# Nine z buffers, three spreads of each kind, and new prices in the planner of a one-core scan, attention and expert kernel

## The chip, the cores and the metric

The kernel runs on one core of a Trainium2 chip. The metric is the device time of one execution in microseconds (us); for a kernel that was run several times it is the median of the runs. Beside the times there is one profiled execution, and everything that is said of single instructions comes from it.

## The reference, cut to what matters

The input x has 4 batches of 384 channels and 32 x 32 positions. Layer 0 is a selective scan in four directions over the 1024 positions; layer 1 is windowed attention followed by a mixture of four experts, of which two serve each token. All numbers are float32.

```
# layer 0, per batch, direction k, channel d, state n (16 states):
dt = softplus(dt_rank @ dt_w + bias)               # time steps
h[l] = h[l-1] * exp(dt[l] * A) + (dt[l] * u[l]) * B[l]
y[l] = sum over n of h[l] * C[l]                   # then four directions are merged,
x = x + gelu(layernorm(merged y + D * u))
# layer 1, per token:
t = t + attention(layernorm(t))                    # 6 heads, causal window of 64
t = t + sum over 2 of 4 experts: gate * (gelu(ln(t) @ w1 + b1) @ w2 + b2)
```

## The kernel before, in words

**The scan.** The 384 channels are cut into 3 tiles of 128 and each tile into 4 blocks of 32 channels. One scan instruction works on 128 partitions (32 channels times 4 states) by 1024 positions, so a block of 32 channels takes 4 *slots* (`NG`), one for each group of 4 states, and the whole kernel 768 slots: 4 batches, 4 directions, 12 blocks, 4 groups. The slots alternate between the two blocks of a pair: `place_of` puts slots 0, 2, 4, 6 of eight in one block and 1, 3, 5, 7 in the other. A slot goes through these steps, each a generator in the code:

- `spread` loads, for each block, two *spreads* from DRAM by a DMA of 512 KB on SyncE's queue: the time steps dt (buffers `dts`) and dt times u (buffers `dtu`, printed in the profile as `dts` too), each row repeated for the four states.
- `times_b` (GpSimd): z = dtu spread times B. It takes a z buffer from the stock `zs_` and may be at most `AHEAD` = 3 slots in front of the scans.
- `decay` (ScalarE): dA = exp(dts spread times A), into one of two PSUM buffers.
- `scan` (VectorE): the recurrence over z and dA.
- `times_c`: the product with C, either on GpSimd, in place in z (`z<-z,bc`), or on VectorE, from PSUM (`z<-dA,bc`). Which it is depends, at planning time, on whether GpSimd's clock in the plan is behind VectorE's by enough.
- `fold_y` (TensorE): sums the four states of a channel by a product with the matrix `fold`, for pairs of slots; then the z buffers are free again.

`time_steps` computes the dt (products `ps_dt`, then ScalarE and VectorE) some 40 slots before they are needed.

**The rest.** As soon as a batch's scans are folded, `tokens` runs its 8 token tiles (norms, attention), then `route` sorts tokens by expert, and `experts` runs 19 *expert blocks* of 128 rows for each batch: 36 products `ps_hid`, 12 gelu activations and 12 products `y_ff`, with the weights loaded from DRAM. `combine` gathers the two experts' rows. Batch b's layer 1 lies beside the scans of the batches after it. What is left of layer 1 after the last scan runs by itself.

**What sets the order.** A planner written in the kernel (`Machine`) runs all generators against a model of the engines before anything is built. Each instruction that a generator yields gets a price from `Engine.ask`; `Machine.choose` picks, on the engine that is free first, the instruction with the smallest ready time plus bias. Biases are `EARLY` (-6), none (the scan chain) or `LATER` (+6, the experts). For TensorE, `account` also keeps a book of work in windows of 3.413 us and stretches a price by `COLD` = 1.9 when the last window had little. The result is one fixed program for each engine. On the chip the engines and SyncE's DMA queue run their programs in order and wait for one another by semaphores; so the prices change nothing on the chip but the order, and who does the second product and the copies.

`settled` holds a generator back until the planned write of a tile lies at most `SOON` ahead.

The prices that the change touches stand in `Engine.ask`: products with 32 output rows are the folds, products with under 32 input rows are the time steps `ps_dt`, and `act` is ScalarE.

Buffers are handed out by `Stock.take` and `Stock.give`, first free first used. At the end of the scans the z, dtu and dts buffers, 15 in all before and after, are given to the stock of rows.

Of the kernel before, what the change touches and what calls it, by code (L numbers as in the profile page):

```python
# [17 lines left out]
P = 128  # L18
B, D, HH, WW = 4, 384, 32, 32
L = HH * WW  # L20
# [22 lines left out]
HID_RANK = 2  # L43
GELU_BIAS = EARLY
FAVOUR = 1.0
TILES, EPS, NZ = 3, 1e-5, 7
CORES = 1
NEG = -1.0e30

# [80 lines left out]
class Engine:  # L130
# [23 lines left out]
    def ask(self, op, a, k):  # L154
        aps = [v for v in list(a) + [v for n, v in k.items() if n not in ("out", "accum_out")] if hasattr(v, "tensor")]
        if "out" in k:
            outs, ins = [k["out"]], aps
        else:
            outs, ins = aps[:1], aps[1:]
        if op == "value_load":  # L160
            outs, ins = [], aps
        if op == "tensor_tensor_reduce":
            outs, ins = outs + ins[-1:], ins[:-1]
        if k.get("accum_out") is not None:
            outs = outs + [k["accum_out"]]
        for v in list(k.values()):
            if isinstance(v, bass.IndirectOffsetOnAxis):
                ins = ins + [v.ap]
        n = max(v.free_size() if callable(v.free_size) else v.free_size for v in (outs if op == "matmul" else outs + ins))
        size, table = 0, None  # L170
        if "dma" in op:
            size = max(_nbytes(v) for v in outs + ins[:1])
            if op == "indirect_dma_start":
                size = P * D * 4
            cost = dict(pool=1.0, act=0.38, sp=0.48)[self.name]
        elif self.name == "pe":
            cost = max(n, 122) * (0.00088 if op == "transpose" else 0.00176)
            if outs[0].shape[0] == 32:
                cost = 0.01 + 0.00022 * n
            if ins[0].shape[0] < 32:  # L180
                cost *= 0.6
        elif self.name == "act":
            cost = 0.08 + 0.00085 * n + 0.1 * sum(hasattr(k.get(v), "tensor") for v in ("bias", "scale"))
            cost += 0.19 if "accum_out" in k else 0.0
            table = TABLES.get(a[2]) if op == "activation" else None
        elif self.name == "pool":
            cost = 0.1 + 0.0022 * n
        elif self.name == "sp":
            cost = 1.5
        else:  # L190
            cost = 0.17 + 0.00198 * n if "scan" in op else 0.14 + 0.00105 * n
            if n < 256 and not any(v.space == PSUM for v in outs + ins):
                cost += 0.5
        asked = Op(self.name, outs, ins, cost, table, size)
        if self.name == "pe":
            asked.work = cost * min(ins[0].shape[0], P) / P if outs[0].shape[0] > 32 else 0.5 * cost
        return asked


def _nbytes(ap):  # L200
    n = 4
    for s in ap.shape:
        n *= s
    return n
# [6 lines left out]
class Machine:  # L211
# [42 lines left out]
            t = max(t, r + (HOP if e != eng else 0.0))  # L254
        return t

    def settled(self, *tiles):

        names = [ap.tensor.name for ap in tiles]
        return lambda: max(self.written.get(n, (0.0, None))[0] for n in names) <= self.t + SOON  # L260

    def account(self, op, start):
        e = op.eng
# [103 lines left out]


PATIENCE = 3.0
SOON = 0.5  # L370
WINDOW, COLD = 3.413, 1.9
MARGIN, QUEUES = 1.0, ("sp",)

# [3 lines left out]
def conv_attn_hybrid(  # L377
# [89 lines left out]
    m = Machine(nc)  # L467
# [41 lines left out]
    work = ctx.enter_context(tc.tile_pool(name="work", bufs=1))  # L509
    rp = ctx.enter_context(tc.tile_pool(name="rp", bufs=2))  # L510
    zs_ = Stock(m, work, "z", NZ, [P, L])
    dtus, dts = (Stock(m, work, n, 4, [P, L]) for n in ("dtu", "dts"))
    bs_, cs_ = (Stock(m, work, n, 4, [P, L]) for n in ("rb", "rc"))
    rows = Stock(m, work, "row", NROW, [P, D])
    xbs, xbts, hss, ybs = (
# [38 lines left out]
    def place_of(s):  # L554

        return s // SP * 2 + s % 2, s % SP // 2
# [280 lines left out]
    def times_c(s, h, on_pool):  # L837
        n, g = place_of(s)
        i = blocks[n][0]
        yield lambda: (i, g, 1) in bcs  # L840
        if on_pool:
            yield from pool.tensor_tensor(zs[s], zs[s], bcs[i, g, 1], ALU.mult)
        else:
            yield from dve.tensor_tensor(zs[s], h, bcs[i, g, 1], ALU.mult)
            das_.give(h)
        if n % NB == NB - 1:
            cs_.give(bcs.pop((i, g, 1)))
        ready.add(s)

    def scan():  # L850

        for s in range(NSLOT):
            n, g = place_of(s)
            i = blocks[n][0]
            yield lambda: s in zs and s in das
            z, da = zs[s], das.pop(s)
            on_pool = count_of["times"] >= min(s + AHEAD, NSLOT) and m.clock["pool"] < m.clock["dve"] + LEAD
            h = z if on_pool else da
            if turns[i][1] >= 2:
                yield from dve.tensor_tensor_scan(  # L860
                    h[:, ::-1], da[:, ::-1], z[:, ::-1], 0.0, ALU.mult, ALU.add
                )
            else:
                yield from dve.tensor_tensor_scan(h, da, z, 0.0, ALU.mult, ALU.add)
            count_of["scan"] = s + 1
            if s % SP == 0:
                m.spawn(fold_y(n), EARLY)
            if on_pool:
                das_.give(da)
                m.spawn(times_c(s, h, True))  # L870
            else:
                yield from times_c(s, h, False)
        ended.append(True)
        yield lambda: len(das_.free) == 2
        for stock in (banks, ybank):
            stock.free.append(das_.free.pop(0))
        for stock, n in ((zs_, NZ), (dts, 4), (dtus, 4)):
            yield lambda: len(stock.free) == n
            rows.free += stock.free
            stock.free = []  # L880
# [3 lines left out]
    def fold_y(n):  # L884


        i, t, j = blocks[n]
        b, k = turns[i]
        rows_y = ydr[b][t, j : j + 2].rearrange("j r l -> (j r) l")
        prev = yield from yps.take("yp")  # L890
        yield from sp.dma_start(prev, rows_y)
        ps = None
        for g in range(NG):
            s = n // 2 * SP + 2 * g
            yield lambda: s in ready and s + 1 in ready
            pair = zs[s], zs[s + 1]
            yield m.settled(*pair)
            mm = Calls()
            if ps is None:
                ps = yield from banks.take("ps_y", 0)  # L900
            for n_z, z in enumerate(pair):
                for h in range(2):
                    if k % 2:
                        rhs = z.rearrange("p (w h) -> p w h", h=HH)[:, :, ts(h, HH // 2)]
                    else:
                        rhs = z[:, ts(h, LH)]
                    q = 32 * (2 * n_z + h)
                    mm.matmul(ps[q : q + 32, :], fold, rhs, start=g == 0, stop=g == NG - 1)
            yield from pe.all(mm)
            zs_.give(zs.pop(s), zs.pop(s + 1))  # L910
        yield from dve.tensor_tensor(prev, ps, prev, ALU.add)
        if k == LAST_BY_COLUMNS:
            yield from act.copy(
                ps.rearrange("p (h w) -> p w h", w=WW), prev.rearrange("p (w h) -> p w h", w=WW)
            )
            yield from act.copy(prev, ps)
        banks.give(ps)
        yield from sp.dma_start(rows_y, prev)
        yps.give(prev)
        folded[b] = folded.get(b, 0) + 2  # L920
        if folded[b] == KG * NB:
            have.add(("scan", b))
# [553 lines left out]
    with tc.manual_schedule():  # L1476
        for b in range(B):
            m.spawn(group_norm(b), EARLY)
        for gen in (turn_loads(), time_steps(), state_rows(0), state_rows(1), spread(1), spread(0)):
            m.spawn(gen, EARLY)  # L1480
        for gen in (decay(), times_b(), scan()):
            m.spawn(gen)
        m.spawn(layer1(), EARLY)
        for gen in (prepare(), mixture()):
            m.spawn(gen, LATER)
        m.run()
# [54 lines left out]
```

## Time and profile before

| | us |
|---|---|
| three runs | 4078.01, 4080.3, 4070.57 |
| median | 4078.01 |
| the profiled execution | 4065.49 |
| its span, first to last instruction | 4063.8 |
| busy in the span: TensorE, VectorE, GpSimd, ScalarE | 3014.8, 2878.0, 2855.7, 2432.7 |

PE is TensorE's matmul, PEld its weight loads, DVE is VectorE, ACT ScalarE, POOL GpSimd, and SPq SyncE's DMA queue. Tiles are printed as output<-inputs. A group of instructions is shown with its count, its busy time and the mean duration of one in ns. Waits are named by the engine that waited and by what ended the wait. The busy shares are means over the whole span; the kernel has stretches with different limits, so they have to be read by stretches. The first scan starts at 104.1 us and the last ends at about 3140 us. The groups with the most time of the scan chain are:

| group | count | mean ns |
|---|---|---|
| POOL z<-dts,bc (first product) | 768 | 2358 |
| DVE scans, into dA and into z | 393 and 375 | 2288 and 2276 |
| POOL z<-z,bc (second product) | 375 | 2356 |
| DVE z<-dA,bc (second product) | 393 | 1221 |
| ACT dA<-dts,a (decay) | 768 | 1116 |
| ACT table loads | 388 | 1283 |

### The profile page before, as it was taken

To read this page: it belongs to the slowest core of one execution; us is meant where nothing else is said; L and a number is where in the kernel's file an instruction comes from. 1 tells how busy PE (TensorE), PEld (TensorE's weight loads), DVE (VectorE), ACT (ScalarE), POOL (GpSimd) and SP (SyncE) were. 2 spreads that over 40 slices of the span, in tenths; PEclk is the share of its full clock that TensorE was granted. 3 is DMA by queue.
4 is the path that set the end of the run, shared out by engine and by line. 5 is a ranking of instruction groups with operands and counts; after the bars stand their busy time and mean duration, and the time that the engine had idled before them with its cause. 6 is when DMAs were issued, how large, how long until landed. Compare 5 with 4: busy or idle time off the path is not lost. (4 is left out here: it accounts for less than half of the span.)

```text
span 4063.8 us, 49234 instructions
## 1 busy us (share of the span) xinstructions
PE 3014.8 (74%) x15856; PEld 1854.0 (46%) x15856; DVE 2878.0 (71%) x3064; ACT 2432.7 (60%) x3979; POOL 2855.7 (70%) x1490
## 2 busy tenths in 40 slices
PE   3554455576674888677777786767799999998998
PEld 1000000043441455445454444444466788887886
DVE  2999999998889888888888889888897232101001
ACT  3554455476774798777776787877777345222221
POOL 1999989989897789999987899899997110101001
PEclk8555566577775899878877787887799999998997
DMA  5565564634345989464668795664569754998995
GB/s 200 203 250 209 217 209 151 209 109 162 114 154 184 382 315 355 164 229 140 215 209 283 268 358 195 230 197 171 190 243 337 240 170 142 345 335 295 315 317 193
DMA packets 368570, 935.11 MB, mean 230 GB/s; under 512 B 48372, under 2 KB 160120, under 8 KB 368312
## 3 DMA queue, kind: packets, MB, share of 16 engines
q1 hardware_dynamic: 360120, 906.79, 63.6%
q0 software_dynamic: 8192, 25.17, 1.8%
q8 instruction: 126, 2.06, 0.2%
q14 instruction: 132, 1.08, 0.1%
HBM read 786.39 MB, written 164.30 MB: 234 GB/s over the span
## 5 line engine op out<-in xcount | busy, mean ns | idle before, releaser
L141 POOL TENSOR_TENSOR z<-dts,bc 128x1024 f32<-128x1024 f32 x768 | 1792.2, 2358 | 177.7 <-PE ps_y L152 95.3
L141 ACT ACTIVATE dA<-dts,a 128x1024 f32<-128x1024 f32 x768 | 851.1, 1116 | 485.5 <-DVE z L141 456.6
L152 PE MATMUL ps_y<-z,fold 128*32 128x512 f32 x3072 | 734.9, 806 | 536.1 <-POOL z L141 253.6
L141 DVE TENSOR_TENSOR_SCAN dA<-dA,z 128x1024 f32<-128x1024 f32 x393 | 899.1, 2288 | 107.6 <-ACT dA L141 88.6
L141 POOL TENSOR_TENSOR z<-z,bc 128x1024 f32<-128x1024 f32 x375 | 879.6, 2356 | 102.6 <-DVE z L141 99.7
L141 DVE TENSOR_TENSOR_SCAN z<-dA,z 128x1024 f32<-128x1024 f32 x375 | 843.8, 2276 | 41.2 <-ACT dA L141 39.4
L152 PEld LDWEIGHTS ps_hid<-xbt,w_sb 128*128 128x128 f32 x5472 | 682.1, 201 | 132.5 <-issue 25.7
L152 PE MATMUL ps_hid<-xbt,w_sb 128*128 128x128 f32 x5472 | 702.0, 286 | 38.0 <-ACT dt L141 19.4
L152 PE MATMUL y_ff<-w_sb,hs 128*128 128x384 f32 x1824 | 659.7, 500 | 19.2 <-ACT hs L141 15.2
L141 ACT ACTIVATE hs<-ps_hid,bb 128x128 f32<-128x128 f32 x912 | 270.5, 366 | 457.1 <-PE ps_hid L152 351.6
L152 PEld LDWEIGHTS ps_y<-z,fold 128*32 128x32 f32 x3072 | 95.1, 123 | 971.4 <-POOL z L141 466.2
L141 ACT ACT_TABLE_LOAD x388 | 497.8, 1283 | 17.2 <-issue 3.6
L141 DVE TENSOR_TENSOR z<-dA,bc 128x1024 f32<-128x1024 f32 x393 | 479.8, 1221 | 13.0
L152 PEld LDWEIGHTS y_ff<-w_sb,hs 128*128 128x128 f32 x1824 | 331.7, 195 | 240.5 <-issue 47.5
L141 POOL DMA_INDIRECT cb<-ysdr,idx x64 | 61.7, 963 | 441.6 <-issue 281.7
L141 DVE COPY xbt<-ps_xb 128x384 f32<-128x384 f32 x39 | 21.7, 556 | 407.7 <-PE ps_xb L152 407.7
L152 POOL TENSOR_TENSOR rn<-rn,half 128x1 f32<-128x1 f32 x96 | 52.5, 547 | 265.6 <-DVE rn L152 256.2
L141 POOL DMA_INDIRECT xsdr<-tks,idx x64 | 63.9, 999 | 168.9 <-DMA xsdr<-tks,idx 119.5
L152 PE MATMUL ps_dt<-xd,dtw_sb 12*128 12x512 f32 x192 | 99.8, 856 | 45.9 <-ACT dt L141 19.2
L152 PE MATMUL ps_o<-v,pt 128*128 128x64 f32 (+1 forms) x720 | 110.1, 315 | 19.6 <-DVE tt L141 7.2
L141 ACT COPY dt<-ps_sp 128x512 f32<-128x512 f32 x96 | 56.0, 584 | 113.5 <-DVE e L141 113.2
L152 PEld LDWEIGHTS ps_o<-v,pt 128*128 128x128 f32 (+1 forms) x720 | 104.9, 227 | 29.4 <-DVE tt L141 7.7
(189 smaller groups left out, 3219.4 us busy)
## 6 DMA issues: line engine op xcount, KB each, us to landing
w_sb<-wl SPq DMA_DIRECT2D x608, 576.0 KB
dts<-dtr SPq DMA_DIRECT2D x384, 512.0 KB
bc<-xdr SPq DMA_DIRECT2D x128, 512.0 KB
ub<-udr SPq DMA_DIRECT2D x48, 512.0 KB
dtr<-e SPq DMA_DIRECT2D x48, 512.0 KB
dtr<-dt SPq DMA_DIRECT2D x48, 512.0 KB
yp<-ydr SPq DMA_DIRECT2D x96, 256.0 KB
ydr<-yp SPq DMA_DIRECT2D x96, 256.0 KB
```

The costliest lines, as they stand in the source:

```text
L141: return getattr(self.real, op)(*a, **k)
L152: getattr(self.real, op)(*a, **k)
```

## The change

There are nine z buffers in place of seven, and three buffers for each kind of spread in place of four, so the bytes in SBUF stay the same. Four prices of the planner go up: the folds, the factor for the time-step products, ScalarE's fixed and per-element price, and the share of a fold that counts as TensorE's work. `settled` takes its limit as an argument, with the same value as before (the plan's time plus 0.5).

```diff
-TILES, EPS, NZ = 3, 1e-5, 7
+TILES, EPS, NZ, SURE = 3, 1e-5, 9, -0.5
...
             if outs[0].shape[0] == 32:
-                cost = 0.01 + 0.00022 * n
+                cost = 0.02 + 0.0004 * n
             if ins[0].shape[0] < 32:
-                cost *= 0.6
+                cost *= 0.9
         elif self.name == "act":
-            cost = 0.08 + 0.00085 * n + 0.1 * sum(hasattr(k.get(v), "tensor") for v in ("bias", "scale"))
+            cost = 0.1 + 0.00088 * n + 0.1 * sum(hasattr(k.get(v), "tensor") for v in ("bias", "scale"))
...
-            asked.work = cost * min(ins[0].shape[0], P) / P if outs[0].shape[0] > 32 else 0.5 * cost
+            asked.work = cost * min(ins[0].shape[0], P) / P if outs[0].shape[0] > 32 else 0.7 * cost
...
-    def settled(self, *tiles):
+    def settled(self, *tiles, sure=-0.5):
...
-        return lambda: max(self.written.get(n, (0.0, None))[0] for n in names) <= self.t + SOON
+        return lambda: max(self.written.get(n, (0.0, None))[0] for n in names) <= self.t - sure
...
-SOON = 0.5
...
-    dtus, dts = (Stock(m, work, n, 4, [P, L]) for n in ("dtu", "dts"))
+    dtus, dts = (Stock(m, work, n, 3, [P, L]) for n in ("dtu", "dts"))
...
-        for stock, n in ((zs_, NZ), (dts, 4), (dtus, 4)):
+        for stock, n in ((zs_, NZ), (dts, 3), (dtus, 3)):
...
-            yield m.settled(*pair)
+            yield m.settled(*pair, sure=SURE)
```

## The prediction

> **What bounds the kernel now.** I read the page's slices first, to see that the span has two regimes; then a table by stretches cut at the first and last scan; then the waits of VectorE and GpSimd inside the first stretch, to see which engine leads there; then the y_ff tile by stretches, to price an expert block.
>
> The page, engines and slices (each digit is a tenth of busy time in one fortieth of the span):
>
> ```profile
> PE   3554455576674888677777786767799999998998
> DVE  2999999998889888888888889888897232101001
> POOL 1999989989897789999987899899997110101001
> ```
>
> VectorE and GpSimd are both near full until slice 31 and almost empty after it; TensorE is then full. The table by stretches, columns as its header says:
>
> ```profile
> core 0: us, PE busy (x) PEld busy (x) DVE busy (x) ACT busy (x) POOL busy (x), PEclk, DMA share, GB/s
> 104.00:780.00 676.00, 344.38 (x875) 49.92 (x874) 650.43 (x446) 353.95 (x387) 637.38 (x278) 0.56 0.58 204
> ...
> 3140.00:4064.00 924.00, 879.12 (x5479) 714.09 (x5477) 141.25 (x447) 279.79 (x818) 90.49 (x121) 0.96 0.76 262
> 104.00:3140.00 3036.00, 2103.84 (x10312) 1127.01 (x10312) 2710.41 (x2564) 2119.26 (x3123) 2749.99 (x1344) 0.76 0.63 221
> ```
>
> So there is a scan stage of 3036 us, in which GpSimd works 90.6% and VectorE 89.3% of the time and TensorE has 932 us to spare, and a tail of 924 us, in which TensorE works 95%. Who leads in the scan stage (waited for: total us, times, longest):
>
> ```profile
> DVE dA L141 <- ACT dA L141: 88.6, 68, 3.8
> DVE z L141 <- ACT dA L141: 39.4, 35, 3.6
> DVE dA L141 <- POOL z L141: 12.5, 9, 6.3
> POOL z L141 <- DVE z L141: 99.7, 44, 13.3
> POOL z L141 <- PE ps_y L152: 95.3, 50, 10.0
> ```
>
> VectorE hardly waits for GpSimd (12.5 us) but 128 us for ScalarE's decays; GpSimd waits 99.7 us for scans and 95.3 us for sums that hold the z buffers. VectorE leads and GpSimd follows closely. The price of an expert block, from y_ff (24 records a block, since each of its 12 products leaves two):
>
> ```profile
> 1396.90:1578.40 181.50, 63.40 (x174) 31.47 (x174) 0.53 (x1) 2.86 (x6) 0.97 0.92 347
> 1770.60:1974.80 204.20, 16.10 (x42) 8.12 (x42) 0.00 (x0) 0.98 (x2) 0.81 0.52 178
> 3845.00:3974.00 129.00, 67.23 (x192) 34.02 (x192) 0.00 (x0) 3.83 (x8) 1.00 0.93 319
> ```
>
> In the tail 192 records, eight blocks, take 129.0 us: 16.1 us each, with nothing to hide them. The first two stretches hold 48 scans each. One has over seven blocks and lasts 181.5 us, the other not two and lasts 204.2 us. So blocks laid beside scans cost the scans nothing visible; what slows them is the work of the token tiles.
>
> **What the change moves.** It is three edits: the planner's prices, the buffers, and a threshold written differently (time plus 0.5 before, time minus -0.5 after: nothing). The planner writes each engine's program once, so its instructions can be counted before running.
>
> 1. Expert blocks leave the scan stage. Before the last fold of a z pair, TensorE's program holds 1269 hidden and 420 output products now, and 1017 and 336 after. A block has 36 and 12, so both say 7 blocks. The prices suggest why: a fold of 512 columns rises from 0.12 to 0.22 us in the planner's book and the time-step products by half, so TensorE's plan is fuller and what has a late bias waits. The total of products is unchanged, 8576. Cost: 7 x 16.1 = 113 us in the tail. The cover they lose is TensorE's spare 932 us of the scan stage. Bounds: if they filled the tail's own 45 us of idle, 68 us; if each cost what the whole tail costs per block that lies in it now, 924 / 40.75 = 22.7 us, 159. I take 113, the row of pure blocks, which they will be.
>
> 2. The last two steps of one token tile and the routing of batch 2 also fall behind the last scan: 9 transposes and small products of the tile and 6 of a shifted combine come, 3 of the projection go: 12 products, 24 records of about 0.28 us, 7 us. Routing's own chain is covered by the blocks of batch 1 that are now left over.
>
> 3. The scan's second product. VectorE's share falls from 393 to 372, GpSimd's rises from 375 to 396. GpSimd: 21 x 2.356 = +49 us; 2 of the 21 come after the last scan's product and 10 indirect transfers leave the stage, so +34 there. VectorE: 21 x 1.221 = -26, and routing and copies that go to the tail or to ScalarE take another 21, so -47. As VectorE leads, -47 counts; GpSimd's +34 lies in its 286 us of idle. If that cover is gone, it is +34.
>
> 4. ScalarE. 32 table loads fewer before the last decay, 32 x 1.283 = 41 us, and 81 gelus, 81 x 0.368 = 30 us. ScalarE is 70% busy; what counts is that work standing between two decays beyond 2.9 us each falls by 11%. Of the 128 us that VectorE waits for decays I take 11%: 14. Bounds: nothing to 128.
>
> The Trainium skill (ScalarE: Activation LUTs, What ACT_TABLE_LOAD costs) puts a drain of 1.38 us behind each 1.283 us load. The group of loads here shows 1283 ns and only 17.2 us of idle ahead of 388 of them, so no such drain is seen; by the page term 4 would remove 85 us of ScalarE time instead of 41, still off the path.
>
> 5. Nine z buffers. GpSimd's plan now makes products five or six ahead of its second product (354 of 396 times) where it was mostly five with many at three and four. What it can win is the 95.3 us of waiting for sums; but VectorE waited only 12.5 us for GpSimd. Bounds 0 to 95; I take 10.
>
> 6. Three spreads instead of four. The slots of work alternate between two blocks, so two spreads are always in use, and a buffer's new content can only be requested when its old reader is done. With four, at least 23.6 us of GpSimd work lay between last old and first new reader. With three, the shortest of the 189 gaps has 4.7 us (two products), 26 have under 6 and 59 under 9. On ScalarE the shortest was 10 us; now 83 are under 9. Against it stands the load: matching packets to issues in order, a spread's last packet ends a median 4.3 us after its issue (nine in ten within 6.9), and the issue comes 0.8 us after the buffer is free on the mean, 9.1 at most, since SyncE's queue is in order. 5.1 us against 26 gaps near 5: about 1 us each, and some for the late ones of the others. The trace of before has only 2.1 us of such waiting in the stage. Bounds: 0 (GpSimd idles anyway) to 59 x (9.4 - 4.7) = 277, with 9.4 the two nine-in-ten figures together, 2.5 and 6.9. I take +30, nearer the low end because before's own order with three buffers would have left 29 gaps under 8 us on GpSimd and none under 5 on ScalarE.
>
> The Trainium skill (DMA: Bandwidth & Descriptors, Rules for kernel authors) says to issue a transfer early and wait late, which speaks against this edit. Its fit for a GpSimd-issued transfer, 2.0 us plus bytes over 436 GB/s, would make a spread an estimated 3.2 us and term 6 nearly nothing; the measured 4.3 us decides.
>
> **The sum.** Scan stage: -47 - 14 - 10 + 30 = -41, so 2995 us, in which GpSimd's 2784 us are 93.0%; the first stretch above, without tokens, ran at 637 of 676, 94.3%, so this is reachable but close. Tail: +113 + 7. Together +79. The profiled execution took 4065.5 us (span 4063.8, so 1.7 around it): 4144.5. The median of the runs lies 12.5 us above that execution, 4078.0; I add it: 4157.
>
> **The rivals.** *The scan stage gives back more than the tail takes.* Mechanism: better prices and two more z buffers remove the drift between plan and chip, and GpSimd closes up. Break-even needs the stage to fall by 120, to 2916 us, with GpSimd 95.5% busy; from 2904 it is visibly faster. For it: GpSimd's 195 us of waits for scans and sums are just what these edits aim at. Against it: GpSimd waits because VectorE leads, VectorE loses only 47 us of work, and no stretch I cut reaches 95%. Its time, with a stage of 2880 us: 4078 + 120 - 156 = 4042. Chance 0.11. *No change*: the stage lasts 2904 to 2928 us; 4078. Chance 0.05.
>
> *The spreads become the bound.* Gaps under 9 us meet a late load in most pairs of blocks, ScalarE's decays too, and GpSimd's new work is no longer covered. Stage +100: 4078 + 120 + 100 = 4298. For it: of three buffers one alone is free to load ahead. Against: on GpSimd more than half of the gaps keep over 15 us. Chance 0.10.
>
> *My forecast*: tail +120, stage -100 to +43. Chance 0.74.
>
> **How the numbers follow.** Range: the low end takes a stage of -115 (GpSimd at 95.3%), 4083; the high end +43, from terms 3 and 6 uncovered with half of the VectorE gain, 4241. About 0.11 lie below and 0.10 above. A difference under about 0.3% (12 us) can't be told from none here. Slower: forecast and spreads, 0.84; same 0.05; faster 0.11.
>
> **What would show it.** Right: last scan near 3100 us; a tail near 1040 us with TensorE over 95% and some 48 blocks after the last scan; GpSimd's waits for ps_y well under 95 us; GpSimd or ScalarE waiting for dts<-dtr in tens of us. Wrong: a last scan before 3010 us (terms 3 to 5 too small), one after 3183 (term 6 too small), or blocks of the tail much off 16.1 us.

## The result, and the profile after

The changed kernel takes 4110.95 us (median of five runs, 4098.69 to 4114.01) against 4076.75 us for the kernel before (median of five, 4065.28 to 4080.3). The ratio is 1.0085, with a 95% interval of 1.0071 to 1.0100: slower, as forecast, but by 34 us where the sum had 79. The profiled execution of the change took 4113.96 us.

The page's slices of the change, one fortieth of 4112.3 us each:

```profile
PE   3544445467776597777777877767789999998998
DVE  2999999999988788998898788988881232101001
POOL 1999979999997899999898999999981020101001
```

The two regimes are as before; the scans now end inside slice 30. Cut at the last scan (columns: stretch, its length, then busy time and records of PE, PEld, DVE, ACT and POOL, clock, DMA share and GB/s), and eight blocks of the tail by their y_ff:

```profile
105.00:3072.50 2967.50, 2018.87 (x9585) 1050.47 (x9584) 2682.91 (x2473) 2047.75 (x2992) 2786.64 (x1353) 0.74 0.61 213
3072.50:4112.30 1039.80, 993.54 (x6207) 806.23 (x6205) 164.51 (x530) 305.94 (x907) 99.92 (x134) 0.96 0.79 272
```

```profile
3865.00:3994.00 129.00, 67.23 (x192) 34.02 (x192) 4.46 (x8) 0.00 (x0) 1.00 0.93 319
```

From the first to the last scan's start the stage lasts 2965 us, 69 less than before's 3034, and the tail 1040 us, 116 more than before's 924. GpSimd is busy 93.9% of the scan stage, where 93.0% was forecast. A block of the tail still takes 16.1 us.

The waits in the scan stage of the change (total us, times, longest):

```profile
DVE dA L141 <- ACT dA L141: 88.1, 60, 3.7
DVE z L141 <- ACT dA L141: 30.5, 29, 5.0
DVE dA L141 <- POOL z L141: 17.1, 11, 3.4
POOL z L141 <- DVE z L141: 54.2, 36, 4.8
POOL z L141 <- PE ps_y L152: 21.3, 5, 17.1
POOL z L141 <- DMA dts<-dtr: 12.8, 6, 3.9
ACT dA L141 <- DMA dts<-dtr: 21.2, 9, 5.2
```

GpSimd's wait for sums fell from 95 to 21 us, and its wait for scans from 100 to 54. A wait that before hardly had has come in, for the spreads: 12.8 us on GpSimd and 21.2 on ScalarE.

### The profile page after: what moved, and what is told of

Its sections match the earlier page's. It is cut to its first block, busy times and chain, and to the rows that moved or that the text cites. A ratio compares the mean times of both kernels' runs of the same rounds, so it can differ in the third digit from the quotient of the medians.

```text
span 4112.3 us, 49126 instructions
## 1 busy us (share of the span) xinstructions
PE 3044.4 (74%) x15856; PEld 1869.7 (45%) x15856; DVE 2873.5 (70%) x3056; ACT 2387.3 (58%) x3938; POOL 2901.3 (71%) x1511
## 5 line engine op out<-in xcount | busy, mean ns | idle before, releaser
L152 PE MATMUL ps_y<-z,fold 128*32 128x512 f32 x3072 | 744.4, 814 | 568.2 <-POOL z L141 288.8
L141 POOL TENSOR_TENSOR z<-z,bc 128x1024 f32<-128x1024 f32 x396 | 929.5, 2356 | 60.9 <-DVE z L141 54.2
L141 DVE TENSOR_TENSOR_SCAN dA<-dA,z 128x1024 f32<-128x1024 f32 x372 | 851.2, 2288 | 105.9 <-ACT dA L141 88.1
L141 DVE TENSOR_TENSOR_SCAN z<-dA,z 128x1024 f32<-128x1024 f32 x396 | 889.5, 2275 | 34.4 <-ACT dA L141 30.5
L141 DVE TENSOR_TENSOR z<-dA,bc 128x1024 f32<-128x1024 f32 x372 | 454.4, 1221 | 11.1
L152 POOL TENSOR_TENSOR rn<-rn,half 128x1 f32<-128x1 f32 x96 | 52.7, 549 | 284.6 <-DVE rn L152 283.3
L141 DVE COPY yb<-y_ff 128x384 f32<-128x384 f32 x26 | 14.4, 556 | 180.7 <-PE y_ff L152 179.3
L152 PE MATMUL ps_s<-k,q 64*128 64x192 f32 (+1 forms) x384 | 96.9, 417 | 55.7 <-ACT dt L141 24.4
```

What stands on the lines that cost most here:

```text
L141: return getattr(self.real, op)(*a, **k)
L152: getattr(self.real, op)(*a, **k)
```

## The experiments

Every experiment is an edit of the kernel before, unless the text says that it starts from the full change. "Stage" is the time from the first to the last scan's start in the profiled execution, "tail" what follows the last scan, "blocks" the expert blocks beside the scans on the chip, counted as the `y_ff` records before the last scan, 24 to a block. Before has 3034, 924 and 34.5; the change 2965, 1040 and 28.0.

**The two halves of the change.** The buffers alone:

```diff
-TILES, EPS, NZ = 3, 1e-5, 7
+TILES, EPS, NZ = 3, 1e-5, 9
...
-    dtus, dts = (Stock(m, work, n, 4, [P, L]) for n in ("dtu", "dts"))
+    dtus, dts = (Stock(m, work, n, 3, [P, L]) for n in ("dtu", "dts"))
...
-        for stock, n in ((zs_, NZ), (dts, 4), (dtus, 4)):
+        for stock, n in ((zs_, NZ), (dts, 3), (dtus, 3)):
```

> Only the buffers change (nine z, three spreads of each kind); the planner's prices are those of before. In its programs 34.0 expert blocks stand before the last fold (35.2 before, 28.2 in the full change), so the tail should be 1.25 x 16.1 = 20 us longer than before's 924. Theory A (the scan stage shrank because nine z buffers end GpSimd's wait for sums): stage 50 to 60 us shorter than before's 3034, total about 35 us below before, 4040. Theory B (it shrank because the new prices bring the plan nearer to the chip): stage within 15 us of before, total 10 to 20 us above before, 4090. Theory C (it shrank because seven expert blocks are no longer beside it, 8 to 10 us each): stage about 12 us shorter, total within 10 us of before.

Measured: 4086.4 us, ratio 1.0019 (1.0002 to 1.0035); stage 3036, tail 956, 33.0 blocks. The stage did not move. Theory A is refuted for the pair of edits. The prices alone (the four price lines of the diff):

> Only the prices change; seven z buffers and four spreads of each kind as before. 27.5 expert blocks stand before the last fold, 7.75 fewer than before: tail 7.75 x 16.1 = 125 us longer. Theory A: stage at most 15 us shorter, total 110 us above before, 4187. Theory B: stage 55 to 70 us shorter, total 55 to 70 above before, 4140. Theory C: stage 65 to 75 us shorter, total 50 to 60 above before, and GpSimd's wait for ps_y stays near 95 us.

Measured: 4150.45 us, 1.0165 (1.0143 to 1.0186); stage 2969, tail 1076, 27.0 blocks. The stage is 65 us shorter, as theories B and C had it, though GpSimd's wait for `ps_y` fell from 95 to 71 us where theory C had it stay, and with the buffers' +2 the halves nearly add up to the change's -69. Their tails, +33 and +152, do not add up to +116.

**The spreads by themselves.** Three spreads of each kind, seven z buffers:

```diff
-    dtus, dts = (Stock(m, work, n, 4, [P, L]) for n in ("dtu", "dts"))
+    dtus, dts = (Stock(m, work, n, 3, [P, L]) for n in ("dtu", "dts"))
...
-        for stock, n in ((zs_, NZ), (dts, 4), (dtus, 4)):
+        for stock, n in ((zs_, NZ), (dts, 3), (dtus, 3)):
```

> Seven z buffers and the old prices, but three spreads of each kind: the price of the spreads alone. 34.5 blocks before the last fold, so 12 us of tail. The forecast's term 6: stage 30 us longer, with some 30 to 40 us of GpSimd and ScalarE waiting for dts<-dtr; total 40 above before. The rival that the waits are covered: the same waits, but stage within 10 us of before and total within 20 us.

Measured: 4115.3 us, 1.0093 (1.0067 to 1.0120); stage 3074, tail 936. In this order the stage is 40 us longer, near the forecast's 30, with 22 and 12 us of waiting for spreads on GpSimd and ScalarE. The run with the buffers alone differs from this one only in two z buffers and has 39 us less of stage, of which 16 are less work of VectorE (383 second products in place of 397). GpSimd's waits in the two, this run's first:

```profile
POOL z L141 <- PE ps_y L152: 107.0, 47, 8.9
POOL z L141 <- DMA dts<-dtr: 22.3, 10, 4.4
```

```profile
POOL z L141 <- DMA dts<-dtr: 29.8, 15, 4.6
POOL z L141 <- PE ps_y L152: 9.3, 6, 3.3
```

With nine z buffers the wait for sums goes from 107 to 9 us, and the wait for spreads stays. So in these orders the two buffer edits pay for each other. How far a stage moves from one order to the next without any reason is measured below.

**What a block beside the scans costs.** The experts held until all scans are planned:

```diff
-            yield lambda: b in routed
+            yield lambda: b in routed and count_of["scan"] >= NSLOT
```

> Before's prices and buffers, but the experts may not start until the last scan is planned, so no block stands beside the scans: tail longer by 35 x 16.1 = 567 us or more. What counts is the scan stage. My reading (blocks beside scans cost them nothing): last scan within 30 us of before's 3138. Theory C: 8 to 10 us less for each of 35 blocks, so a last scan 280 to 350 us earlier, 2790 to 2860.

Measured in its one run: 4600.73 us; last scan at 3051.5, stage 2947, tail 1545. 34.5 blocks fewer make 87 us of stage, 2.5 each. Theory C's 8 to 10 are refuted, but so is a cost of nothing. A later start alone, with `>= 400` in the same place:

> Before's prices and buffers, but the experts may not start before scan 400 is planned (their first block stands near scan 310 in before). 26.2 blocks before the last fold, 9 fewer than before, and nothing else touched: tail 9 x 16.1 to 18.5 = 145 to 167 us longer. Over the nine orders with experts seen so far, the stage is about 2639 + 11.9 us for each block beside it. Theory E (the blocks themselves set the pace of the scans): stage 9 x 11.9 = 107 us shorter, 2927. Theory F (blocks and stage length only go together, because a plan that runs layer 1 beside the scans less densely has shorter stages and later experts; a block alone costs the 2.5 us of the run with the experts late): stage 22 us shorter, 3012.

Measured in its one run: 4186.56 us; stage 2995, tail 1083, 25.5 blocks. The stage lies between the two theories, nearer to F's 3012. The cleanest reading is the eighth from scan 288 to 384. Up to there these two runs and before went alike (398, 399 and 401 us for the eighth ahead of it). Before has 9.25 blocks in it, the other two have none. The stretch in before, then with the experts late, then with the late start:

```profile
1178.30:1578.40 400.10, 292.07 (x1572) 173.57 (x1571) 345.36 (x308) 295.72 (x412) 336.06 (x159) 0.82 0.77 287
```

```profile
1180.10:1548.80 368.70, 194.66 (x646) 56.38 (x648) 345.47 (x309) 190.95 (x236) 332.91 (x158) 0.60 0.50 175
```

```profile
1181.10:1555.40 374.30, 193.78 (x646) 56.25 (x648) 345.36 (x309) 191.01 (x236) 332.73 (x158) 0.60 0.50 172
```

VectorE's work is the same to a record, GpSimd's nearly. Only TensorE's and ScalarE's work and the DMA traffic differ, and the stretch is 31 and 26 us shorter: 2.8 to 3.4 us for each block that is gone. In the eighths behind it, where the orders have drifted apart, the run with the experts late is between 50 us shorter and 26 us longer than before, so this price holds for this stretch. VectorE's wait for decays tells by which way. In this stretch before has 23.5 us of it and the two others 4.2 us each; before, then with the experts late:

```profile
DVE dA L141 <- ACT dA L141: 15.0, 9, 3.8
DVE z L141 <- ACT dA L141: 8.5, 8, 2.3
```

```profile
DVE z L141 <- ACT dA L141: 2.7, 2, 2.3
DVE dA L141 <- ACT dA L141: 1.5, 3, 0.9
```

Over the whole stage before had 88.6 and 39.4 us of it; with the experts late:

```profile
DVE dA L141 <- ACT dA L141: 34.6, 39, 3.8
DVE z L141 <- ACT dA L141: 16.6, 16, 3.6
```

So 19 of the 31 us are decays that come late, and it is the blocks' work on ScalarE's queue that is gone from between them. Whether the rest is TensorE's work or the weights' DMA traffic, which left with the blocks, no run tells.

**The prices, and prices that mean nothing.** The fold's price and its share of work alone:

> Of the new prices only the fold's and its share of work, on before's buffers. 29.5 blocks before the last fold, 5.75 fewer: tail 93 us longer; at the 2.5 us a block of the run with the experts late, the stage gives back 14. Theory B: VectorE's waits for TensorE fall from 110 to about 80 us and the stage by 40 or more, total 50 above before. Theory D: stage 14 us shorter, give or take 30, total 80 above, give or take 30.

Measured: 4116.81 us, 1.0097 (1.0062 to 1.0132); stage 2982, tail 1030, 29.2 blocks. VectorE's waits for TensorE fell from 110 to 89 us and the stage by 52: nearer to theory B, and outside theory D's -14 give or take 30. ScalarE's price alone:

> Of the new prices only ScalarE's, on before's buffers. 33.2 blocks before the last fold, 2 fewer: tail 32 us longer. Theory B: VectorE's waits for ScalarE fall from 161 to about 130 us and the stage by 30, total within 10 of before. Theory D: stage 5 us shorter, give or take 30, total 27 above.

Measured: 4083.72 us, 1.0015 (1.0000 to 1.0030); stage 3009, tail 965. The stage fell by 25 us, but VectorE's waits for ScalarE only from 161 to 146, so the means that theory B names carried half of it. Then two edits that tell the planner nothing new. The first:

```diff
-TABLE_LOAD = 1.3
+TABLE_LOAD = 1.29
```

> A price that means nothing: before with the planner's table load at 1.29 us in place of 1.30 (the profile shows 1.283). Its programs hold 31.2 blocks before the last fold, 4 fewer than before. Theory D (any change of a price draws a new order, and stage and blocks scatter): tail 64 us longer, stage anywhere within 40 us of before's 3034, at least 10 away. Theory B (what counts is how near the prices are to the chip): stage within 10 us of before, total 55 to 75 above.

Measured: 4104.34 us, 1.0067 (1.0043 to 1.0092); stage 3003, tail 994, 30.5 blocks. The stage is 31 us shorter, as theory D had it and against theory B's 10; so the 52 us of the fold's price are not by themselves the merit of a better price. The second:

```diff
-HOP = 0.15
+HOP = 0.152
```

> A second price that means next to nothing: the planner's hop between engines at 0.152 us in place of 0.150. 33.2 blocks before the last fold. By the line over the orders seen so far: stage about 3026 give or take 15, tail about 964, total 10 to 20 us above before. If orders of nearly equal prices scatter independently of the blocks, the stage is off that line by more than 30 us.

Measured: 4133.5 us, 1.0123 (1.0093 to 1.0153); stage 3050, tail 975. A hop of 2 ns more costs more than the whole change. It lies 23 us off the line, inside the 30 set as the limit, but the stage moved up with fewer blocks, against the line. To see whether the change keeps apart from such scatter, the same two edits were made on the full change, and two more on before. The first two, table load 1.29 and hop 0.152 on the change:

> The full change with the planner's table load at 1.29 in place of 1.30, a price that means nothing. 26.5 blocks before the last fold, 28.2 in the change. If the change's stage of 2965 us is what its prices and buffers mean, the stage is within 15 us of that and the tail 28 us longer by 1.75 blocks of 16.1: total about 4140. If it is one draw among many, as the same edit on before suggests (31 us of stage), the stage is off by 20 to 40 us either way, total 4110 to 4170.

Measured: 4134.89 us, 1.0133 (1.0113 to 1.0153); stage 2942, tail 1081.

> The full change with the hop between engines at 0.152 in place of 0.150. 28.5 blocks before the last fold, as good as the change's 28.2. If the stage belongs to the change: 2950 to 2980, total within 12 us of 4111. If it is one draw: off by 20 us or more.

Measured: 4161.42 us, 1.0200 (1.0183 to 1.0217). Its 28.0 blocks and 1039 us of tail are those of the change; its stage is 3006, 41 longer:

```profile
104.00:3112.40 3008.40, 2037.36 (x9627) 1051.80 (x9627) 2688.38 (x2496) 2064.88 (x2990) 2783.37 (x1355) 0.73 0.61 210
3112.40:4151.50 1039.10, 991.73 (x6158) 804.25 (x6156) 162.82 (x525) 300.54 (x891) 97.15 (x130) 0.96 0.79 271
```

VectorE's and GpSimd's busy times are the change's to within 6 us, so some 35 of the 41 us are idle: the same work, drawn in another order. Hop 0.16 on before:

> Before with the hop at 0.16 in place of 0.15. 34.2 blocks before the last fold (35.2 in before): tail 16 us longer. If before is a middling draw of its prices, stage within 15 us of 3034 either way and total 4080 to 4110. If before is a lucky one, the total lies above 4095, as with the two such edits seen (4104 and 4134).

Measured: 4085.67 us, 1.0015 (1.0005 to 1.0026); stage 3050, tail 937. Table load 1.31 on before:

> Before with the table load at 1.31 in place of 1.30. 35.0 blocks before the last fold, as in before. If blocks and prices decide, total within 15 us of before. If before is a lucky draw, stage 15 us or more longer, total above 4095.

Measured: 4079.44 us, 1.0007 (0.9996 to 1.0019); stage 3044, tail 926. So five orders from before's prices have ratios of 1, 1.0007, 1.0015, 1.0067 and 1.0123, mean 1.0042; three from the change's have 1.0085, 1.0133 and 1.0200, mean 1.0139. The families overlap, but the means are 0.97% apart, some 40 us. Before is the best of its five, level with the table load of 1.31, and the change the best of its three. The spread inside each family, 0.5 to 0.6%, leaves the 40 us uncertain by about 17 (one standard error), with so few orders. The stages stand further apart: 3003 to 3050 us from before's prices, mean 3036, and 2942 to 3006 from the change's, mean 2971, so 65 us less. The mean tails are 951 and 1053.

**Fewer token tiles, and two tries for a faster version.** Two tiles in flight (`TILES` 2):

> Before's prices and buffers, but two token tiles in flight in place of three. 30.0 blocks before the last fold. Theory F: the eighth of the stage where only token tiles lie beside the scans (scans 192 to 288, 398 us in before and 370 in the full change) falls to 380 or less and the stage to about 2990. Rival (tokens do not matter, the prices do): that eighth within 8 us of 398, stage within 15 us of 3020. The tail is 80 to 90 us longer in both, so totals 4110 and 4145.

Measured: 4140.22 us, 1.0142 (1.0110 to 1.0173); stage 3017, tail 1013. The eighth from scan 192 to 288 fell to 374, as theory F had it; the stage fell by 17, which is the rival's size. So fewer token tiles go with a shorter eighth there, and elsewhere it was given back. The experts' bias at +2, with the buffers of the change:

```diff
-EARLY, LATER = -6.0, 6.0
+EARLY, LATER = -6.0, 2.0
```

> The buffers of the change, the prices of before, and the experts' bias at +2 in place of +6. 36.8 blocks before the last fold, 1.5 more than before and 2.75 more than with the buffers alone: tail 24 us shorter than before. If blocks are worth 16.1 us and the stage stays at the 3036 us of the run with the buffers alone, the total is 24 us under before, 4052, and this is the fastest version. If the stage pays for blocks, 2.5 us each, 4059. If a new order scatters the stage by 30 us, 4030 to 4090.

Measured: 4089.6 us, 1.0026 (1.0011 to 1.0040); stage 3062, tail 912. The tail is 12 us shorter, and the stage took more than that: the total lies at the upper end of the third expectation, that of a new order. TensorE's products at a lower price, with the buffers of the change:

```diff
-            cost = max(n, 122) * (0.00088 if op == "transpose" else 0.00176)
+            cost = max(n, 122) * (0.00088 if op == "transpose" else 0.0016)
```

> The buffers of the change, the prices of before but for TensorE's products, 0.0016 us a column in place of 0.00176 (the tail of before runs a block of 9216 columns in 16.1 us, 0.00175). It was picked because 38.0 blocks stand before its last fold, 2.75 more than before. With blocks worth 18.5 us of tail and costing 4.3 us of stage (the run with the late start), beside the run with the buffers alone: tail about 880 us, stage about 3055, total some 25 us under before, 4050. By the line over all orders, where a block goes with 11.9 us of stage: stage 3080, total 5 to 10 us under before. If the plan's cheaper products make the real ones late and hold the sums up, the stage is 3100 or more and the total above before.

Measured: 4083.06 us, 1.0016 (1.0002 to 1.0029); stage 3098, tail 879. The tail came as expected, to a microsecond or two; the stage was 43 us over the one expectation and 18 over the line, 2 us short of the third one, that cheaper products in the plan make the real ones late; VectorE's waits for TensorE rose from 110 to 148 us. No order that was run is faster than before.

## Why the prediction was right in its direction and wrong in its size

*The tail (terms 1 and 2): right.* 120 us were forecast, 116 measured; 16.1 us a block held in the tail's pure stretch, and what had covered the blocks was the scan stage. That the whole came within 4 us is partly luck: at the same 16.1 us a block, the tail of the prices alone was expected 125 us longer and was 152, that of the fold's price 93 and was 106.

*The scan stage: the terms that were mis-sized.* -41 was forecast, -69 measured; the means of the two families of orders, 65 us apart, say the same with less of the luck of one order. In VectorE's terms, with the tables cut at the last scan, its busy time fell by 27 us (2710.4 to 2682.9), where term 3 had 47, and its idle time fell by 41 us (325.6 to 284.6), where terms 4 to 6 together had let it grow by 6. But 17 us of the busy time look like waiting. One record, `g<-g` of 128 x 3 elements, which takes 0.16 us at the start of before, takes 19.64 us in the change, and ends 0.02 us after a row of GpSimd's instructions that ran without a pause. Here are the record in before and in the change, then the end of that row and what follows it:

```profile
28.44 0.16 DVE L141 SCALAR_TENSOR_TENSOR g<-g 128x3 f32<-128x3 f32 x1 [1.01 <-POOL g L141]
```

```profile
520.12 19.64 DVE L141 SCALAR_TENSOR_TENSOR g<-g 128x3 f32<-128x3 f32 x1
```

```profile
530.51 9.23 POOL L141 TENSOR_TENSOR z<-dts,bc 128x1024 f32<-128x1024 f32 x4
556.80 2.37 POOL L141 TENSOR_TENSOR z<-dts,bc 128x1024 f32<-128x1024 f32 x1 [17.05 <-PE ps_y L152]
```

No scan ran meanwhile, and GpSimd then waited 17 us for sums, most of the 21.3 us that it has in the whole stage. Counted as the wait that it looks like, the record leaves VectorE's work 44 us shorter (second products 25, the rest 19) and its waiting 24 us shorter. So term 3's 47 was nearly right, and the step of the prediction that failed is the waiting, terms 4 to 6: +6 forecast, -24 measured. Term by term:

- Terms 5 and 6, the buffers, were -10 and +30, so +20. The pair moved the stage by +2 on before's prices (3034 to 3036) and by -4 on the new ones (2969 to 2965): 18 to 24 us less than forecast, which is most of the difference. Taken singly, on before's prices, three spreads are +40 and two more z buffers -39. Each of these figures is the difference of two orders, and edits without meaning moved the stage by as much as 41 us; only the pair was measured twice. That nine z buffers end GpSimd's wait for sums is plain (107 to 9 us). Term 5 took VectorE's 12.5 us of direct waiting for GpSimd as a sign that little could be won. VectorE also waits for what comes late by way of ScalarE and TensorE, but which of these waits the z buffers shorten is not shown.
- The reading under the y_ff table, that blocks laid beside scans cost the scans nothing, is wrong. It compared two stretches with different token work. Where only the blocks differ, one costs 2.8 to 3.4 us, so the 6.5 blocks that left would be about 20 us. The sum did not leave all of that out, since term 4's 14 us are for the same blocks' gelus and table loads. And in the change itself VectorE's waits for decays fell by 9 us only, from 128 to 119, so the 20 us cannot be seen there.

How the rest of the waiting divides stays open; it is smaller than what a meaningless edit does. A reading in term 4 also tests less than it says: the 17.2 us of idle lie ahead of the table loads and cannot show a drain behind them. Behind a load the trace of before has a median of 12 ns of idle, so none is seen there either.

Part of the 69 us is visible in the eighth from scan 192 to 288, in which neither kernel has an expert block: before, then the change,

```profile
780.30:1178.30 398.00, 270.02 (x1332) 152.69 (x1329) 346.76 (x401) 274.79 (x466) 362.18 (x195) 0.72 0.42 147
```

```profile
786.00:1156.40 370.40, 249.39 (x1167) 135.12 (x1168) 342.60 (x371) 258.48 (x423) 357.66 (x186) 0.70 0.45 155
```

28 of the 69 us are won there, with VectorE's work 4 us less. The norm records of the trace say what moved: the change runs 18 norms of token tiles beside these scans, before 22. The first batch's 24 norms end at scan 324 in place of 302, so the experts start 24 scans later (349, not 325). That fits one shift in the plan, layer 1 laid less densely beside the scans, which shortens the stage and lengthens the tail; the sum priced only the second. The norms carry a part of it: in all 18 orders the eighth takes 369 to 383 us with 17 to 20 norms and 379 to 407 with 21 or 22. But the table load of 1.31 on before, with 21, already takes 380, so how much of the 28 us is the norms and how much the draw is not shown.

*The offset.* 12.5 us were added because before's profiled execution lay that far under the median of its runs. With five runs it is 11, and the change's execution lies 3 over its median. This alone is 15.5 of the 46 us between 4157 and 4111, the spread of single runs and no mechanism; the stage is 28, the tail 4, and the first scan came 1 us later.

*The rivals.* GpSimd did reach 93.9%, and its waits for scans and sums fell from 195 to 76 us, as the rival of the faster kernel had it; the stage fell by 69 us of the 120 that it needed. The spreads did not become the bound: 34 us of waiting for them.

*What the forecast lacked altogether* is the scatter of the planner. The same prices, with a hop 2 ns longer, give the change 4161 us, which is where the forecast was. A sum made from the counts of one order can't know the idle time that the next order draws, here -31 to +41 us of stage for edits without meaning. The mean of the change's three orders lies 40 us above the mean of before's five; so the change probably has an effect of its own on the total, about half of what was forecast, though eight orders do not fix it well. Its two halves, a longer tail and a shorter stage, stand clearer: 102 and 65 us between the means.

## What to carry to other kernels

Where a planner fixes the order, count what each program holds beside and behind the bounding stage, and price both: work that leaves the stage costs its full time behind it, but what it did to the stage comes back. To price work that lies beside a bound engine, compare stretches that differ in that work alone. Make one or two edits without meaning before reading a difference of one per cent as the merit of a price, and doubt a tuned order first: it may be the best of its neighbours.

## What the runs showed of the hardware that was not expected

A transfer of 512 KB that SyncE issues when its buffer comes free lands a median 4.3 us after the issue, and with three buffers GpSimd and ScalarE waited 34 us for such transfers over 768 slots. Programs that were equal up to a point ran equal on the chip: three orders took 398, 399 and 401 us for the same eighth. A short VectorE instruction can last until GpSimd's unbroken row of products ends, and counts as busy all the while: 19.64 us for 128 x 3 elements in the change, 15.06 us for a copy `k<-k` with the hop of 0.152 on the change. All twelve VectorE records over 4 us in the 18 orders end within 0.15 us of such a row. In the six orders with nine z buffers the longest takes 8.2 to 19.6 us, in the twelve with seven at most 6.6; more buffers may let GpSimd run longer before it must wait, which was not tested.
